# Fused multi-query attention with a residual: the upper query blocks are stored in reversed order, and the opening loads and a few early steps are put in another order

## The chip, the core and the metric

The kernel runs on one core of a Trainium2 chip. The core has five engines that work from instruction queues of their own and wait for each other by semaphores: TensorE (PE in the profile, with its weight loads shown as PEld), VectorE (DVE), ScalarE (ACT), GpSimd (POOL) and SyncE (SP). Here SyncE does nothing but issue DMA transfers, in the order in which the program lists them. The metric is the device time of one execution in microseconds; lower is better. The time shown for the kernel before is the median of three runs.

## The reference

All arrays are float32 apart from the mask. `x` is 64 x 128 x 512: 64 batches of 128 tokens.

```python
xn  = layernorm(x, g_in)
q   = (xn @ Wq) per head * 64**-0.5     # 16 heads of 64
k, v = split(xn @ Wkv)                  # one head of 64, shared by all 16 (multi-query)
k, v = [null_k; k], [null_v; v]         # a null key and value in front, from cond_64[0:2]
sim = q @ k.T + bias                    # bias: a null column, then 16 x 128 x 128
sim = causal mask, then the key mask of the batch
attn = softmax(sim)
out = layernorm((attn @ v, heads side by side) @ Wo, g_out)
return x + out
```

Two facts matter below. The attention is causal: query i uses keys 0 to i and the null key. And it is block-causal in blocks of 32: query block 0 needs key block 0, query block 3 needs key blocks 0 to 3.

## The kernel before

**Groups and steps.** The 64 batches are worked on one at a time in `step(n)`; each step is written out by hand as one order of instructions for all engines (`step_a` for even n, `step_b` for odd n, `last_step` for the last six). The projections are made for a group of four batches (GB = 4): while step n does the attention of batches n to n + 2, it also makes a quarter of the queries, keys and values of the group that is wanted about six batches later (`g, f = divmod(n + 6, GB)`). With f = 3 the group is complete, and its keys and values go through DRAM to the partitions where they are wanted (`keys_T`, `values_spread`), and its key mask is made (`mask_neg`). The query projection and the output projection use seven products of halves in place of eight (`product`, `out_product`).

**Attention of one batch.** Queries of 8 heads by 128 tokens are packed onto 128 partitions as (u, i, q): u is a half of the head pairs, i one of two blocks of 32 queries, q a query in its block. The free dimension holds, for each of 8 heads, 64 keys for the *lower* queries (tokens 0 to 63; constant `LK`) and 128 keys for the *upper* queries (tokens 64 to 127; `UK`). So partition row group s = 2u + i (32 partitions) holds lower query block i and upper query block 2 + i. The order in `region(n)` is: `scores` of the lower half of batch n + 2 (PE, line 515), `scores_add` (DVE, line 528), `values` of batch n (PE, line 606), then `scores` of the upper half of n + 2, which overwrites the same PSUM tile `ps`, and so must wait until `scores_add` has read it. `scores_add` itself adds onto the tile `s` that `bias_add` (POOL, line 494) has filled with bias and mask.

**values.** The transposed softmax weights `sb` hold, in each row group, six blocks of 32 keys: slots 0 and 1 for the lower query block, 2 to 5 for the upper one. For key block j and row group s a matmul with 32 rows and 64 columns of weights is issued for each half r of the heads, at `tile_position=(s * Q, r * DH)`: eight small tiles of the array. Where both query blocks of the row group need key block j (`both`) it streams 256 columns, otherwise 128 for the upper block alone. A row group with i = 0 needs 1 + 3 key blocks, one with i = 1 needs 2 + 4. `values_out` (ACT, line 622) moves the four PSUM tiles `po` to `oT`.

**Where the token order is set.** `xT[g]` holds the normalised tokens with features on partitions. For the first two groups `norm_T` makes it by PE transposes and one ACT copy from PSUM for each batch (line 290); for the others `tokens_T` does 32 x 32 transposes on DVE (line 299), and `tokens_out` and `tokens_in` go through DRAM. Queries, keys and values all come from `xT`, so its order of tokens is theirs. The bias is loaded once by `load_bias` into `biasp` in the order of the queries, and `causal` (POOL, line 196) writes -1e38 where a key lies after its query.

**Opening.** Batches 0 to 3 are loaded first, then the weights; `load_second` issues what follows on SP's queue. Of each batch, `norm_stats`, `norm_apply` and `norm_T` must be done before its keys and values (`kv_mm`, `kv_out`). In PSUM, `norm_T` and `kv_mm` take turns on the two buffers of `ps_w`. `norm_apply` is on DVE for batches 0 to 3 and on ACT from batch 4 on (line 278). `rstd` is made on POOL (line 257), whose queue also holds `causal`.

Of the kernel before, what the change touches and what calls it, by code (L numbers as in the profile page):

```python
# [17 lines left out]
def kernel(  # L18
# [76 lines left out]
    ROW = 1 + NL + N + 1  # L95
    LK, UK = slice(1, 1 + NL), slice(1 + NL, 1 + NL + N)
    assert NQ == GB and NQ == KC
    EPS = 1e-5
    NEG = -1.0e38
    XB = 3  # L100
# [36 lines left out]
    def load_mask(g):  # L137
        m8s[g] = gp.tile([P, TOK], U8, tag="m8", name=f"m8_{g}")
        nc.sync.dma_start(
            out=m8s[g],  # L140
            in_=mask[g * GB : (g + 1) * GB].rearrange("b n -> (b n)").partition_broadcast(P),
        )
# [23 lines left out]
    nc.sync.dma_start(out=wkv, in_=w_kv.rearrange("(kc p) f -> p kc f", p=P))  # L166

    def load_second():
        load_bias(1)
        nc.sync.dma_start(out=nbh, in_=null_bias.partition_broadcast(P))  # L170
        nc.sync.dma_start(
            out=nkv, in_=cond[0:2].rearrange("r d -> (r d)").partition_broadcast(P)
        )
        load_bias(0)
        load_mask(0)
        for r in range(2):
            nc.sync.dma_start(
                out=nv2[r * DH : (r + 1) * DH, :], in_=cond[1].unsqueeze(1)
            )
        for m in range(XB + 1, 2 * GB):  # L180
            load_x(m)
        load_mask(1)

    def load_bias(u):
        rows = slice(u * DH, (u + 1) * DH)
        bias_r = attn_bias.rearrange("(u f r) i j -> u r i f j", u=2, r=2)[u]
        for r in range(2):
            rf = slice(r * NF, (r + 1) * NF)
            nc.sync.dma_start(out=biasp[rows, rf, LK], in_=bias_r[r, 0:DH, :, 0:NL])
            nc.sync.dma_start(out=biasp[rows, rf, UK], in_=bias_r[r, DH:N])  # L190

    def causal(u):

        rows = slice(u * DH, (u + 1) * DH)
        for keys, base in ((LK, 0), (UK, DH)):
            nc.gpsimd.affine_select(
                biasp[rows, :, keys],
                biasp[rows, :, keys],
                pattern=[[0, R8], [-1, keys.stop - keys.start]],
                compare_op=ALU.is_ge,  # L200
                fill=NEG,
                base=base,
                channel_multiplier=1,
            )
# [77 lines left out]
    def norm_T(m):  # L282
        g, t = divmod(m, GB)
        if t == 0:
            xT[g] = gp.tile([P, GB, KC, N], FP, tag="xT", name=f"xT_{g}")
        xh = xs.pop(m)
        pt = ps_w.tile([P, KC, P], FP, tag="w", name=f"pxT_{m}")
        for kc in range(KC):
            nc.tensor.transpose(pt[:, kc, :], xh[:, kc * P : (kc + 1) * P], ident)
        nc.scalar.copy(xT[g][:, t], pt)  # L290

    xbs = {}

    def tokens_T(m):

        g, t = divmod(m, GB)
        if t == 0:
            xbs[g] = hp.tile([P, NQ, KC, NQ, Q], FP, tag="xb", name=f"xb_{g}", bufs=1)
        nc.vector.transpose(
            xbs[g][:, :, :, t, :].rearrange("p j c q -> p c j q"),  # L300
            xs.pop(m).rearrange("p (c j k) -> p c j k", c=KC, k=Q),
        )

# [34 lines left out]
    def kv_out(m, pkv):  # L338
# [7 lines left out]
            ALU.subtract,  # L346
        )

    def values_spread(g):

        vd = dp.tile([P, GB * DH], FP, tag="vd", name=f"vd_{g}")
        nc.sync.dma_start(out=vd, in_=kvts[g][:, 1].rearrange("p t d -> p (t d)"))
        vr[g] = hp.tile([P, NQ, GB, DH], FP, tag="vr", name=f"vr_{g}")
        src = vd.rearrange("(j p) e -> p j e", p=Q)
        for s in range(NQ):
            nc.sync.dma_start(
                out=vr[g][s * Q : (s + 1) * Q].rearrange("p j t d -> p j (t d)"),
                in_=src,
            )

    def keys_T(g):

        kb = hp.tile([P, 2, GB, Q], FP, tag="kb", name=f"kb_{g}", bufs=1)
        nc.vector.transpose(
            kb,
            kvts[g][:, 0].rearrange("p t (c k) -> p c t k", k=Q),
        )
        kd = dp.tile([P, 2, GB * Q], FP, tag="kd", name=f"kd_{g}")
        nc.sync.dma_start(
            out=kd.rearrange("p c e -> p (c e)"), in_=kb.rearrange("p c t q -> p (c t q)")  # L370
        )
        kT[g] = hp.tile([P, NQ, GB, Q], FP, tag="kT", name=f"kT_{g}")
        src = kd.rearrange("(i p) c e -> c p i e", p=Q)
        for s in range(NQ):
            nc.sync.dma_start(
                out=kT[g][s * Q : (s + 1) * Q].rearrange("p i t q -> p i (t q)"),
                in_=src[s % 2],
            )
# [90 lines left out]
    def q_out(g, c, toks, tag, name=None):  # L469
        lo = toks.start // N  # L470
        o = q_part(g, c, lo, lo + 2)
        p = prod[tag].rearrange("p (t h i) -> p t h i", t=2, h=2)
        if name is None:
            nc.scalar.copy(o, p)  # L474
        else:
            k = kept.pop(name).rearrange("p (t h i) -> p t h i", t=2, h=2)
            nc.vector.tensor_tensor(o, p, k, ALU.add)  # L477
# [108 lines left out]
    def values(b):  # L586

        g, t = divmod(b, GB)
        sb = sbs.pop(b)
        po = [  # L590
            (ps_w if s % 2 else ps_q).tile(
                [P, 2, NF, Q], FP, tag="w" if s % 2 else "ac"[s // 2], name=f"po_{b}_{s}"
            )
            for s in range(NQ)
        ]
        for j in range(NQ):
            for s in range(NQ):
                i = s % 2
                if j > 2 + i:
                    continue  # L600
                quad = slice(s * Q, (s + 1) * Q)
                both = j <= i
                slots = slice(j, j + 3, 2) if both else slice(2 + j, 3 + j)
                for r in range(2):
                    rows = slice(r * DH, (r + 1) * DH)
                    nc.tensor.matmul(  # L606
                        po[s][rows] if both else po[s][rows, 1:2],
                        vr[g][quad, j, t, :],
                        sb[quad, slots, r * NF : (r + 1) * NF, :],
                        start=(j == 0),  # L610
                        stop=True,
                        skip_group_check=(j > 0),
                        tile_position=(s * Q, r * DH),
                    )
        pos[b] = po

    def values_out(b):

        oT[b] = bp.tile([P, NC, N], FP, tag="oT", name=f"oT_{b}")
        for s, po in enumerate(pos.pop(b)):  # L620
            u, i = divmod(s, 2)
            nc.scalar.activation(  # L622
                oT[b][:, u * NF : (u + 1) * NF, :].rearrange(
                    "p f (h i q) -> p i h f q", h=2, i=2
                )[:, i],
                po,
                AF.Identity,
                bias=nv2,
            )
# [150 lines left out]


    def weights_q(kc):
        if kc in (2, 0):
            nc.vector.tensor_scalar(
                wq[:, kc, :], wq[:, kc, :], gin8[:, kc : kc + 1], None, ALU.mult
            )
        else:
            nc.scalar.activation(
                wq[:, kc, :], wq[:, kc, :], AF.Copy, scale=gin8[:, kc : kc + 1]
            )  # L790
# [32 lines left out]
    def step_a(n):  # L823
# [4 lines left out]
        first, third = paired(p12), paired(p4)  # L828
        e, nb = n + 1, n + 2
        soft = 0 < n  # L830
        if q and f == 0 and g + 1 < NG:
            load_mask(g + 1)
        if third:
# [109 lines left out]
        if n == -2:  # L943
            scores(1, 1)
            scores_add(1, 1)
            late_max.append(1)
        for m in (n + 12, n + 13):
            if m < B and n:
                load_x(m)

    def step_b(n):

# [52 lines left out]
        if q:  # L1005
            product(g, f, 7, ps_q, "a", start=False)
            keep("a", "u3")
            q_out(g, HC + f, hi_t, "c", "u3")
            if kv_late:
                kv_out(n + 6, keys_values())  # L1010
            if n == 1:
                out_mm(0)
# [29 lines left out]
        if q:  # L1042
            product(g, f, 4, ps_q, "a", start=False)
            q_out(g, HC + f, lo_t, "a")
            if f == 3:
                keys_T(g)
                values_spread(g)
                if g < NG:
                    mask_neg(g)
        if second:  # L1050
            out_product(p, 3, ps_y, "Y", start=False)
# [102 lines left out]
    norm_stats(3)  # L1154
    q_half(0, 0)
    norm_apply(2)
    norm_T(2)
    q_half(1, 0)
    norm_apply(3)
    norm_T(3)  # L1160
    weights_kv()
    norm_stats(4)
    norm_apply(4)
    q_half(2, 0)
    causal(1)
    norm_stats(5)
    norm_apply(5)
    null_shift(1)
    q_half(3, 0)
    norm_T(4)  # L1170
    for m in range(GB):
        kv_out(m, kv_mm(m))
    norm_stats(6)
    norm_stats(7)
    norm_nmr(6)
# [18 lines left out]
    weight_sum(4)  # L1194
    for c in range(4):
        q_half(c, 1)
    load_late()
    load_x(8)
    load_x(9)
# [75 lines left out]
```

## Time and profile before

| | |
|---|---|
| median of three runs | 1103.41 us (1102.82 to 1104.4) |
| the profiled execution, its own time | 1104.52 us |
| its span from first to last instruction | 1102.7 us |
| busy, share of the span | PE 98%, PEld 82%, DVE 73%, ACT 63%, POOL 64% |
| DMA moved | 105.03 MB, mean 95 GB/s |
| costliest PE groups of the chain that ended last | query products (line 456, by tile) 17%, 8% and 5%; output products (line 689) 16%, 7% and 4%; scores 9%; values 7% |
| granted clock of PE | 0.50 from 27.0 to 30.0 us, from 107.5 to 110.5 us and from 134.7 to 137.7 us; 1.00 in nearly all of the rest |

How to read it: times in the views are microseconds from the start of the span. A group of instructions is shown as line, engine, operation, tile written and tile read, sizes (partitions x elements), how many, and their time. One float32 matmul of the program stands in the trace as two records. A bracket such as `[4.50 <-ACT x L278]` says that the engine had been idle for 4.50 us, and that the instruction of that engine and line ended the wait. In a table of stretches, the columns after the length are the busy times of PE, PEld, DVE, ACT and POOL with their instruction counts, then the granted clock of PE as a share of full speed, the busy share of the DMA engines, and GB/s.

### The profile page before, as it was taken

How to read it: one execution, taken by the hardware profiler on the slowest of the kernel's cores; microseconds unless marked ns; L12 is line 12 of the kernel's file. 1: busy time of each engine (PE TensorE's matmuls, PEld its weight loads, DVE VectorE, ACT ScalarE, POOL GpSimd, SP SyncE). 2: the span in 40 equal slices, each digit the busy share in tenths (PEclk: the TensorE clock that was granted, in tenths of full speed). 3: DMA queues.
4: the chain of work that ended last, by engine and by line, in shares of the span. 5: the costliest groups of instructions: out<-in, count | busy, mean ns of one | idle time of the engine just before them, and what ended most of it. 6: DMA issues, size and time to landing. Idle time of an engine off the chain costs nothing.

```text
span 1102.7 us, 29987 instructions
## 1 busy us (share of the span) xinstructions
PE 1077.4 (98%) x11780; PEld 900.2 (82%) x11780; DVE 800.9 (73%) x1545; ACT 694.9 (63%) x2779; POOL 702.1 (64%) x517
## 2 busy tenths in 40 slices
PE   7999999999999999999999999999999999999997
PEld 6876788888888888888888888888888888888653
DVE  4667578786787878678687787878678787657772
ACT  3355566666766666666666676666676666567682
POOL 2465757676675766757586675767667576665572
PEclk9999999999999999999999999999999999999999
DMA  7414242333334242333324234233333424111211
GB/s 198 139 44 120 77 117 76 112 90 111 82 100 122 70 120 78 118 97 92 105 80 133 69 90 133 70 118 89 112 84 99 121 67 125 58 59 41 68 60 67
DMA packets 67980, 105.03 MB, mean 95 GB/s; under 512 B 8448, under 2 KB 32640, under 8 KB 66048
## 3 DMA queue, kind: packets, MB, share of 16 engines
q1 hardware_dynamic: 67024, 102.07, 31.1%
q8 instruction: 92, 1.51, 0.6%
q10 hardware_dynamic: 816, 1.05, 0.3%
q14 instruction: 48, 0.39, 0.1%
HBM read 67.45 MB, written 35.65 MB: 93 GB/s over the span
## 4 chain that ended last, share of the span: by engine, by line
PE 86%; DVE 7%; ACT 4%; DMA 2%; issue 1%; POOL 0%; SPq 0%; DVEq 0%; ACTq 0%
PE pa L456 17%; PE pyX L689 16%; PE ps L515 9%; PE pc L456 8%; PE pyY L689 7%; PE po L606 7%; PE pkv L327 6%; PE py L636 5%; PE pw L456 5%; PE pyw L689 4%; DVE mneg L485 3%; ACT s L542 3%; PE pq L405 2%; ACT x L278 1%; DVE s L528 1%; DMA x<-in_x_dram 1%
## 5 line engine op out<-in xcount | busy, mean ns | idle before, releaser
L542 ACT ACTIVATE s<-s,nmax 128x65 f32<-128x65 f32 (+1 forms) x1024 | 372.5, 370 | 6.1 <-DVE nmax L533 6.1
L563 POOL TENSOR_TENSOR s<-s,rinv 128x512 f32<-128x512 f32 (+1 forms) x128 | 189.2, 1478 | 184.1 <-DVE rinv L559 177.3
L494 POOL TENSOR_TENSOR s<-biasp,mneg 128x1552 f32<-128x1552 f32 x64 | 206.1, 3220 | 105.4 <-DVE sb L578 103.0
L542 ACT ACTIVATION_READ_ACCUMULATOR s<-s,nmax 128x1 f32 x1024 | 197.6, 193 | 0.0
L622 ACT ACTIVATE oT<-po,nv 128x256 f32<-128x256 f32 x256 | 100.2, 474 | 139.5 <-PE po L606 139.5
L528 DVE TENSOR_TENSOR s<-ps,s 128x512 f32<-128x512 f32 (+1 forms) x128 | 119.9, 936 | 64.9 <-PE ps L515 64.9
L689 PE MATMUL pyX<-wT,oT 128*128 128x256 f32 x672 | 163.2, 386 | 0.0
L689 PEld LDWEIGHTS pyX<-wT,oT 128*128 128x128 f32 x672 | 124.5, 191 | 22.8 <-issue 4.8
L515 PEld LDWEIGHTS ps<-kT,qT 64*64 64x64 f32 x4096 | 90.9, 133 | 40.7 <-issue 29.6
L456 PE MATMUL pa<-xS,wq 128*128 128x256 f32 x480 | 123.5, 380 | 0.0
L533 DVE TENSOR_REDUCE nmax<-s 128x8 f32<-128x520 f32 (+1 forms) x128 | 122.1, 954 | 1.4
L515 PE MATMUL ps<-kT,qT 64*64 64x64 f32 (+1 forms) x4096 | 115.1, 250 | 5.6 <-DVE s L528 4.1
L578 DVE STREAM_TRANSPOSE sb<-s 128x1536 f32<-128x1536 f32 x64 | 113.5, 1773 | 8.0 <-POOL s L563 3.8
L456 PEld LDWEIGHTS pa<-xS,wq 128*128 128x128 f32 x480 | 91.4, 191 | 12.6
L606 PE MATMUL po<-sb,vr 32*64 32x128 f32 (+1 forms) x3584 | 99.7, 322 | 0.3 <-ACT qT L474 0.3
L606 PEld LDWEIGHTS po<-sb,vr 32*64 32x64 f32 x3584 | 79.4, 131 | 10.9 <-DVE y L760 0.8
L467 ACT COPY ku<-pa 128x256 f32<-128x256 f32 x120 | 44.7, 372 | 65.4 <-PE pa L456 64.1
L477 DVE TENSOR_TENSOR qT<-pc,ku 128x256 f32<-128x256 f32 x120 | 49.7, 414 | 42.6 <-ACT ku L467 35.3
L327 PE MATMUL pkv<-wkv,xT 128*128 128x128 f32 x512 | 73.6, 290 | 1.0 <-ACT xT L290 1.0
L327 PEld LDWEIGHTS pkv<-wkv,xT 128*128 128x128 f32 x512 | 67.3, 199 | 8.0 <-issue 5.2
L278 ACT ACTIVATE x<-x,nmr,rstd 128x512 f32<-128x512 f32 x60 | 48.5, 814 | 32.6 <-DVE nmr L265 31.7
L456 PE MATMUL pc<-xT,wS 128*128 128x256 f32 x240 | 62.0, 381 | 3.6 <-DVE qT L477 3.5
(95 smaller groups left out, 1926.7 us busy)
## 6 DMA issues: line engine op xcount, KB each, us to landing
x<-in_x_dram SPq DMA_DIRECT2D x64, 256.0 KB
res<-in_x_dram SPq DMA_DIRECT2D x64, 256.0 KB
out_dram<-y SPq DMA_DIRECT2D x64, 256.0 KB
xd<-xb SPq DMA_DIRECT2D x14, 1024.0 KB
xT<-xd SPq DMA_DIRECT2D x56, 256.0 KB
vr<-vd SPq DMA_DIRECT2D x64, 128.0 KB
kT<-kd SPq DMA_DIRECT2D x64, 64.0 KB
kd<-kb SPq DMA_DIRECT2D x16, 128.0 KB
```

The costliest lines, as they stand in the source:

```text
L327: nc.tensor.matmul(pkv, xT[g][:, t, kc, :], wkv[:, kc, :], start=(kc == 0), stop=(kc == KC - 1),)
L456: nc.tensor.matmul(prod[tag], w[:, kc, f * P : (f + 1) * P], t[:, :, kc, :], start=(start and kc == 0), stop=(kc == HK - 1), skip_group_ch ...
L494: nc.gpsimd.tensor_tensor(S[b], biasp, mneg[:, t].unsqueeze(1).broadcast_to([P, R8, ROW]), ALU.add,)
L515: nc.tensor.matmul(pv[u * DH : (u + 1) * DH, r, f, :], qT[g][rows, f, t, hf, u], kT[g][rows, 0 : nk // Q, t, :], start=True, stop=True,)
L528: nc.vector.tensor_tensor(sv, pss.pop((b, hf)), sv, ALU.add)
L533: nc.vector.tensor_reduce(nmax[b][:, hf], S[b][:, :, WITH_NULL[hf]], AX.X, ALU.max, negate=True)
L542: nc.scalar.activation(row, row, AF.Exp, bias=nmax[b][:, hf, k : k + 1], accum_out=rsum[b][:, hf, k : k + 1],)
L563: nc.gpsimd.tensor_tensor(sv, sv, rinvs.pop((b, hf)).unsqueeze(2).broadcast_to([P, R8, sv.shape[2]]), ALU.mult,)
L578: nc.vector.transpose(sb.rearrange("p j e q -> p e j q"), S[b][:, :, 1 : ROW - 1].rearrange("p e (j k) -> p e j k", k=Q),)
L606: nc.tensor.matmul(po[s][rows] if both else po[s][rows, 1:2], vr[g][quad, j, t, :], sb[quad, slots, r * NF : (r + 1) * NF, :], start=(j == 0),
L622: nc.scalar.activation(oT[b][:, u * NF : (u + 1) * NF, :].rearrange("p f (h i q) -> p i h f q", h=2, i=2)[:, i], po, AF.Identity, bias=nv2,)
L689: nc.tensor.matmul(prod[key], h[:, c, :], w[:, c, :], start=(start and c == 0), stop=(c == HC - 1), skip_group_check=not start,)
```

## The change

The upper queries of a row group are stored in reversed block order: row groups with i = 0 get lower block 0 and upper block 3, those with i = 1 get lower block 1 and upper block 2. Each then needs five key blocks. `values` issues its 14 pairs of matmuls in a list written out for that. The order is made where `xT` is written (three ACT copies in place of one for the first eight batches; another place in the DVE transpose for the others), `load_bias` and `causal` follow it in more pieces, keys and values are brought back to the order of the tokens on their way through DRAM (three DMAs in place of one for each), and `values_out` puts the blocks back with another stride.

Apart from that, batch 4 is loaded at the head of `load_second`, batches 5 to 7 ahead of the second bias half, and the null value later; one of the four query weight scalings goes from ACT to DVE; `norm_T(2)` and `norm_T(3)` stand one projection later and `null_shift(1)` after the keys and values of the first group; the mask of group 1 is made earlier in step 1; and in `step_a` the two loads of `x` stand at the beginning and no longer at the end.

```diff
+    PLACE = 0, 1, 3, 2
     def load_second():
+        load_x(XB + 1)
         load_bias(1)
...
+        for m in range(XB + 2, 2 * GB):
+            load_x(m)
         load_bias(0)
         load_mask(0)
+        load_mask(1)
+
+    def load_null_value():
         for r in range(2):
             nc.sync.dma_start(
                 out=nv2[r * DH : (r + 1) * DH, :], in_=cond[1].unsqueeze(1)
             )
-        for m in range(XB + 1, 2 * GB):
-            load_x(m)
-        load_mask(1)
...
-            nc.sync.dma_start(out=biasp[rows, rf, UK], in_=bias_r[r, DH:N])
+            for i, at in enumerate((N - Q, N - 2 * Q)):
+                nc.sync.dma_start(
+                    out=biasp[u * DH + i * Q : u * DH + (i + 1) * Q, rf, UK],
+                    in_=bias_r[r, at : at + Q],
+                )
     def causal(u):
-        rows = slice(u * DH, (u + 1) * DH)
-        for keys, base in ((LK, 0), (UK, DH)):
+        for rows, keys, base in (
+            (slice(u * DH, (u + 1) * DH), LK, 0),
+            (slice(u * DH, u * DH + Q), UK, N - Q),
+            (slice(u * DH + Q, (u + 1) * DH), UK, N - 2 * Q),
+        ):
...
-        nc.scalar.copy(xT[g][:, t], pt)
+        for at, to, n in ((0, 0, 2), (3, 2, 1), (2, 3, 1)):
+            nc.scalar.copy(
+                xT[g][:, t, :, to * Q : (to + n) * Q], pt[:, :, at * Q : (at + n) * Q]
+            )
...
-            xbs[g][:, :, :, t, :].rearrange("p j c q -> p c j q"),
+            xbs[g][:, :, :, PLACE[t], :].rearrange("p j c q -> p c j q"),
...
+    def to_tokens(out, places):
+        for at, to, n in ((0, 0, 2), (2, 3, 1), (3, 2, 1)):
+            nc.sync.dma_start(
+                out=out[to * Q : (to + n) * Q], in_=places[at * Q : (at + n) * Q]
+            )
...
-        nc.sync.dma_start(out=vd, in_=kvts[g][:, 1].rearrange("p t d -> p (t d)"))
+        to_tokens(vd, kvts[g][:, 1].rearrange("p t d -> p (t d)"))
...
-        for j in range(NQ):
-            for s in range(NQ):
-                i = s % 2
-                if j > 2 + i:
-                    continue
+        order = [(0, s) for s in range(NQ)] + [(1, s) for s in range(NQ)]
+        order += [(2, 0), (2, 2), (3, 0), (2, 1), (3, 2), (2, 3)]
+        for j, s in order:
+            i = s % 2
...
+            blocks = slice(i, 4 - i, 3 - 2 * i)
                 oT[b][:, u * NF : (u + 1) * NF, :].rearrange(
-                    "p f (h i q) -> p i h f q", h=2, i=2
-                )[:, i],
+                    "p f (s q) -> p s f q", q=Q
+                )[:, blocks],
...
     def weights_q(kc):
-        if kc in (2, 0):
+        if kc != 1:
...
     def step_a(n):
+        for m in (n + 12, n + 13):
+            if m < B and n:
+                load_x(m)
...
-        for m in (n + 12, n + 13):
-            if m < B and n:
-                load_x(m)
     def step_b(n):
...
+            if n == 1:
+                mask_neg(g)
...
                 values_spread(g)
-                if g < NG:
+                if n > 1:
                     mask_neg(g)
...
     q_half(0, 0)
     norm_apply(2)
+    norm_apply(3)
+    q_half(1, 0)
     norm_T(2)
-    q_half(1, 0)
-    norm_apply(3)
-    norm_T(3)
     weights_kv()
     norm_stats(4)
     norm_apply(4)
     q_half(2, 0)
+    norm_T(3)
     causal(1)
     norm_stats(5)
     norm_apply(5)
-    null_shift(1)
     q_half(3, 0)
     norm_T(4)
     for m in range(GB):
         kv_out(m, kv_mm(m))
+    null_shift(1)
...
+    load_null_value()
     load_late()
```

## The prediction

> **What bounds the kernel now.** I read the page first, then the stretches, then the order of PE's work in time, and last the chain.
>
> ```profile
> PE 1077.4 (98%) x11780; PEld 900.2 (82%) x11780; DVE 800.9 (73%) x1545; ACT 694.9 (63%) x2779; POOL 702.1 (64%) x517
> 237.00:499.00 262.00, 261.48 (x2946) 224.95 (x2945) 201.43 (x397) 174.22 (x697) 175.19 (x129) 1.00 0.34 99
> 27.00:30.00 3.00, 2.22 (x10) 2.22 (x11) 1.52 (x3) 0.72 (x2) 0.00 (x0) 0.50 0.00 0
> 107.50:110.50 3.00, 3.00 (x11) 2.55 (x10) 2.93 (x6) 1.34 (x9) 0.20 (x1) 0.50 0.40 106
> 134.70:137.70 3.00, 3.00 (x9) 2.38 (x8) 1.49 (x4) 1.86 (x9) 2.94 (x2) 0.50 0.31 131
> ```
>
> In the steady part PE is idle for 0.5 of 262 us: there only less PE time counts. Elsewhere there are three stretches at half clock; these are PE's waits ahead of them:
>
> ```profile
> 24.62 0.66 PE L289 MATMUL pxT<-ident,x 128*128 128x128 f32 x4 [4.50 <-ACT x L278]
> 27.78 5.03 PE L327 MATMUL pkv<-wkv,xT 128*128 128x128 f32 x24 [0.98 <-ACT xT L290]
> 105.74 1.10 PE L515 MATMUL ps<-kT,qT 64*64 64x128 f32 x32 [2.45 <-DVE s L528]
> 133.40 1.13 PE L456 MATMUL pc<-xT,wS 128*128 128x256 f32 x4 [2.29 <-DVE qT L477]
> ```
>
> The attention of two neighbouring steady steps, 24 and 25:
>
> ```profile
> 483.38 0.69 PE L515 MATMUL ps<-kT,qT 64*64 64x64 f32 x32
> 484.00 1.56 PE L606 MATMUL po<-sb,vr 32*64 32x256 f32 x56
> 485.49 1.10 PE L515 MATMUL ps<-kT,qT 64*64 64x128 f32 x32
> 501.19 1.56 PE L606 MATMUL po<-sb,vr 32*64 32x256 f32 x56
> 502.87 1.10 PE L515 MATMUL ps<-kT,qT 64*64 64x128 f32 x32
> ```
>
> `values` takes 1.49 us from its start to the next start at 484.00, and 1.68 at 501.19. The second is a step with f = 3; the chain tells what ended it:
>
> ```profile
> 499.32 2.89 DVE mneg L485 x2
> 502.22 0.61 DVE s L528
> 502.83 0.04 issue
> 502.87 1.10 PE ps L515 x32
> ```
>
> The mask on DVE makes `scores_add` late by 0.2 us. In the other steps nothing waits there.
>
> **Part 1, values.** Four full matmuls of 256 columns take 1.73 us in the chain (1.69 ns a column). A row group with i = 1 streams 2 x 256 + 2 x 128 = 768 columns per half r: 1.30 us, plus 0.19 to the next form, is the 1.49 seen. So both halves and all four row groups run side by side, and the longest row group sets the time; the single records agree, with 0.216 us between passes of 256 columns in one tile while eight tiles run. After the change each row group has 640 columns: 128 x 1.69 = 0.216 us less, to 1.27. Bounds: 0, if the new order lets one group wait for another, and 0.41, if the 0.19 to the next form went too. I take 0.216: the tiles' starts in the trace do not follow the program's order across row groups, so none waits for another.
>
> [...]
>
> Where it counts: of 64 batches not in the 12 steps with f = 3 from 5 to 49 (1.68 us there; DVE's chain begins at PE's `pyX` of the same step, so PE only waits 0.4 in place of 0.2), nor in batches 60 and 61, where the chain runs over DVE and ACT from 1058.3 to 1068.1. 50 x 0.216 = 10.8 us. `values_out` starts 0.43 nearer to PE's end, since row group 0 ends last too; ACT's four moves (1.57 us) still end over 1 us ahead of the `kv` and `pa` that want the buffers.
>
> **Part 2, the opening.** Before, PE is done with the fourth query tile at 20.14 and reaches the fifth at 32.81: 12.67 us for 0.44 + 4 x 0.87 = 3.92 us of work. `x` of batch 4 is issued at 18.79, behind eight bias DMAs and two of the null value (2.39 us), and read at 21.67. Now it is issued at 6.9 in place of the first bias DMA, behind `wkv`, which lands at 13.7; so by about 14.4. Then:
> - DVE scales a third weight (0.75 us) when it lands (10.83): `norm_stats(2)` starts at 11.6, not 10.46, and all to `wkv` 1.16 later (15.76). PE does not see it: its first query tile waits for ACT's scaling at 13.32 as before.
> - Batch 4, with the gaps it had from 21.67 to 24.56: statistics 15.76, POOL 17.0 to 17.55, ACT 17.85 to 18.65. PE, with two transposes moved back, reaches `norm_T(4)` at 19.85, no wait; first keys 20.3 to 21.17.
> - The second keys need the buffer that ACT's `xT` copies of batch 4 free. On ACT `norm_apply(5)` is ahead of them; it needs POOL's `rstd`, behind `causal(1)`, now in three pieces (0.66 + 1.09 + 1.09, to 20.35). From the end of `causal` to PE it was 25.25 to 27.78, 2.5 us; three copies take about 0.2 more than one (0.58 us for 128 x 512, 0.37 for 256, so 0.27 for 128, partly overlapped): 23.05. PE waits 1.9 us and is done with the keys at 25.65.
> - `null_shift(1)` (1.92) now lies between `kv_out` and `norm_stats(6)`, which starts at 27.9; ACT's `norm_apply(6)` ended 3.06 after that start (33.06 to 36.12): 30.95. PE is there at 29.55: waits 1.4. `norm_T(6)` at 31.0 is 5.7 us ahead of the 36.7 before.
> - Behind it, mask, `bias_add(0)` (4.04) and DVE's weight sums (1.2 + 4.1 + 2.2) end at about 43, when the first `scores` end (48.56 less 5.7): level. The three `kd` DMAs and `kT` land by 37. The null value (2.39 on SP) delays `wo` and batches 8 and 9, wanted some 9 us later. From there PE, ACT and DVE follow each other as before.
>
> Gain 5.7. Bounds: 8.75, all of the excess; and about 2, if both waits bring half clock again (1.7 each, as in part 3).
>
> **Part 3, step 1.** Mask 1 moves from 101.8 to 94.5, ahead of a wait of 3.56 us on DVE (to 100.35) that takes up its time; POOL's last read of the old mask ends at 92.8. `values` to `scores`, 4.01 us at 101.73, becomes 1.49 (counted above down to 1.27): 2.5, and the half clock from 107.28 to 110.69 goes: 3.41 / 2 = 1.7. Sum 4.2; at least 2.5.
>
> [...] The records here show half clock after 2.45 and 2.29 us, and they decide.
>
> **Part 4, loads of x.** In step 2 they were issued at 122.5, behind the store, and landed at 131.9 (DVE waits 2.06 and 1.45 for them, PE 2.29). Now they are issued after `vr` (110.0), need no buffer that is still in use, and land ahead of 125. 2.4 plus 1.7 = 4.1. Bounds 0 (another wait there) and 4.5. In later steps they free only DVE waits that PE does not see.
>
> **Part 5, what is added.** Keys and values back to token order: three DMAs for one, twice in each of 16 groups. SP's queue moves by 2 x 0.33 + 2 x 0.43 = 1.5 us, and `kv_out` of the next group, which overwrites the source, must wait for the third `vd`:
>
> ```profile
> 502.92 0.43 SPq L352 DMA_DIRECT2D vd<-kvt  x1
> 506.11 1.73 SPq L356 DMA_DIRECT2D vr<-vd  x4
> 508.60 0.28 DVE L342 TENSOR_TENSOR kvt<-pkv,nkv 128x128 f32<-128x128 f32 x1
> ```
>
> `vr` starts when `vd` has landed, `kvt` 2.5 us later; over the groups the margin is 2.06 to 3.9. So 1.5 is hidden, 0.5 left: cost 0. `kT` and `vr` are wanted a step or more later. Four more bias DMAs and the last `causal` pieces lie under PE's work of the opening.
>
> **Part 6, the tail.** PE's wait at 1066.5 (1.61 us, no half clock) grows by 2 x 0.216 to 2.04. Waits of 1.61 and 2.29 lie on two sides of what halves the clock; 2.04 is nearer to the second: cost 1.7, or 0.
>
> **Sum.** 10.8 + 5.7 + 4.2 + 4.1 - 1.7 = 23.1 us. The profiled execution took 1104.52 (span 1102.7 and 1.8 around it): 1081.4. The median is 1.1 below it: 1080.3.
>
> **Rivals.**
> - *The opening trades its wait for others.* For: two waits of 1.4 and 1.9 are foreseen, both behind POOL's and DVE's queues. At half clock or with DMAs landing later it gives 0 to 3: 1083 to 1086.
> - *`values` does not get shorter where it counts*: another queue order, or DVE takes PE's place in more steps (it is busy for 77% of the steady part). Against: in the other steps `scores` start 0.2 us after the last matmul starts, with no wait. All lost, and with it the tail's longer wait: 1080.3 + 10.8 - 1.7 = 1089.4, and less where only some steps lose it.
> - *Slower: `kv_out` waits for `vd` on DVE.* Behind it DVE holds `q_out` and with that PE's buffers. It has to cost 23.1 / 14 = 1.7 us in each of 14 groups; from a wait of that size half clock doubles it, some 1104 to 1128. The third `vd` would have to land 4 us later than now, not 1.5.
> - *Better*: no wait at 21.2, none in the tail: 1073 to 1077.
>
> **How the numbers follow.** Forecast (1077 to 1083) 0.54; opening 0.18; values 0.14; slower 0.05; better 0.09. 1075 to 1089.5 leaves out the slower case, some of the better and a little of the third: under 0.15, as the chances are themselves rough. A measurement of this kernel can tell about 0.2%, 2.2 us; faster 0.94, same 0.01, slower 0.05.
>
> **What would show it.** 1.27 us from `values` to `scores` in steps without a mask, 1.68 with f = 3; no idle PE from 20.1 to 21.1, then waits of 1 to 2 us; clock 1.00 in all of 25 to 138; no `kvt` on DVE ended by a DMA. It is wrong if `values` stays at 1.49, or if PE shows new waits in each group.

## The result, and the profile after

The changed kernel takes 1092.03 us (median of four runs, 1090.72 to 1093.44); the kernel before, on the same chip, 1103.91 us. The ratio is 0.9894, 95% interval 0.9875 to 0.9912: faster by 11.9 us, about half of the 23.1 that the prediction summed up, and outside its range (1075 to 1089.5). The profiled execution took 1093.44 us, with a span of 1090.7 us, 12.0 less than before.

The page's busy times of the changed kernel:

```profile
PE 1072.2 (98%) x11780; PEld 896.5 (82%) x11780; DVE 797.6 (73%) x1546; ACT 694.6 (64%) x2794; POOL 703.5 (65%) x519
```

The same stretches that the prediction showed (the first one is chosen anew, where the half clock lies now; columns: length, busy times of PE, PEld, DVE, ACT and POOL, granted clock, DMA share, GB/s):

```profile
23.60:27.00 3.40, 3.33 (x15) 3.33 (x16) 0.29 (x1) 0.01 (x1) 0.00 (x0) 0.50 0.19 26
107.50:110.50 3.00, 3.00 (x16) 2.64 (x15) 1.23 (x5) 2.25 (x12) 3.00 (x2) 1.00 0.51 143
134.70:137.70 3.00, 3.00 (x18) 2.69 (x18) 2.93 (x9) 2.10 (x12) 2.75 (x3) 1.00 0.63 132
237.00:499.00 262.00, 261.46 (x2946) 224.83 (x2946) 201.15 (x398) 174.43 (x698) 175.06 (x130) 1.00 0.33 99
```

The half clock at 107 and at 135 us is gone (the column before the last two is 1.00), PE is as full in the steady part as before, and one window of half clock remains in the opening. PE's order in time, changed kernel, opening:

```profile
20.23 1.06 PE L341 MATMUL pkv<-wkv,xT 128*128 128x128 f32 x8
23.67 4.52 PE L341 MATMUL pkv<-wkv,xT 128*128 128x128 f32 x24 [2.38 <-ACT xT L302]
33.67 0.55 PE L300 MATMUL pxT<-ident,x 128*128 128x128 f32 x3 [1.59 <-ACT x L289]
```

The wait of 4.50 us ahead of the fifth query tile is gone; in its place stand 2.38 us ahead of the second keys and 1.59 us ahead of `norm_T(6)`, the two places that the prediction named. Further on, the same view of the two places that had a wait, `scores` in step 1 and the query product `pc` in step 3:

```profile
98.81 1.55 PE L623 MATMUL po<-sb,vr 32*64 32x256 f32 x56
100.28 1.10 PE L533 MATMUL ps<-kT,qT 64*64 64x128 f32 x32
...
122.22 1.89 PE L707 MATMUL pyX<-wT,oT 128*128 128x256 f32 x8
123.95 1.03 PE L474 MATMUL pc<-xT,wS 128*128 128x256 f32 x4
```

`scores` follow `values` by 1.47 us with no wait, and `pc` has none either. And in the steady part, steps 24 and 25:

```profile
472.58 1.55 PE L623 MATMUL po<-sb,vr 32*64 32x256 f32 x56
474.05 1.10 PE L533 MATMUL ps<-kT,qT 64*64 64x128 f32 x32
...
489.75 1.55 PE L623 MATMUL po<-sb,vr 32*64 32x256 f32 x56
491.44 1.10 PE L533 MATMUL ps<-kT,qT 64*64 64x128 f32 x32
```

This is the surprise. In the step without a mask, `values` takes 1.477 us from its start to the next start, not 1.27; before it took 1.486 (medians over the 64 batches). With f = 3 it stays at 1.68. Worked out from the starts of `values` in both traces, the 12.0 us come from:

| stretch | before | after | gain |
|---|---|---|---|
| start to the first `scores` | 47.88 | 45.06 | 2.8 |
| step 1 (second to third `values`) | 17.93 | 13.86 | 4.1 |
| step 3 (third to fourth `values`) | 21.43 | 17.18 | 4.2 |
| all other steps together | | | 0.9 |

Of the last row, `values` itself makes up about 0.45 us (50 x 0.009); the rest was not followed up.

### The profile page after: what moved, and what is told of

Its sections match the earlier page's. It is cut to its first block, busy times and chain, and to the rows that moved or that the text cites. A ratio compares the mean times of both kernels' runs of the same rounds, so it can differ in the third digit from the quotient of the medians.

```text
span 1090.7 us, 30112 instructions
## 1 busy us (share of the span) xinstructions
PE 1072.2 (98%) x11780; PEld 896.5 (82%) x11780; DVE 797.6 (73%) x1546; ACT 694.6 (64%) x2794; POOL 703.5 (65%) x519
## 4 chain that ended last, share of the span: by engine, by line
PE 86%; DVE 7%; ACT 4%; DMA 2%; issue 1%; POOL 0%; ACTq 0%; SPq 0%; DVEq 0%; POOLq 0%
PE pa L474 18%; PE pyX L707 16%; PE ps L533 9%; PE pc L474 8%; PE pyY L707 7%; PE po L623 7%; PE pkv L341 6%; PE py L654 5%; PE pw L474 5%; PE pyw L707 4%; DVE mneg L503 3%; ACT s L560 2%; PE pq L423 1%; DMA x<-in_x_dram 1%; ACT x L289 1%
## 5 line engine op out<-in xcount | busy, mean ns | idle before, releaser
L764 DVE TENSOR_TENSOR yn<-yn,gob 128x512 f32<-128x512 f32 x56 | 39.2, 700 | 36.3 <-ACT yn L761 36.3
```

## The experiments

The first theory was that the row group whose pair stands last in the list, (2,3), gets its weights late. A record is one entry of the trace, a weight load or a pass (the streaming of one matmul's columns); in batch 24 the 28 float32 matmuls of `values` stand as 56 loads and 56 passes. In the records of batch 24 the last pass of `values` starts at 1.280 us, where 640 columns would have it near 1.075. The rival: 56 passes have a fixed price of 26.4 ns each, whatever their order.

### Other orders of the last pairs

```diff
-        order += [(2, 0), (2, 2), (3, 0), (2, 1), (3, 2), (2, 3)]
+        order += [(2, 0), (2, 1), (2, 2), (2, 3), (3, 0), (3, 2)]
```

> Same matmuls as in the changed kernel, but the last six pairs of values are issued key block by key block, as the loop of the kernel before had them: (2,0), (2,1), (2,2), (2,3), (3,0), (3,2). Theory (what holds values at 1.477 us is the place of the pair (2,3) at the end of the list: its weights are loaded late, and its last pass starts at 1.280 us where 1.075 was due): the pair now stands fourth, values takes 1.28 to 1.40 us from its start to the next form, and the profiled time falls by 4 to 10 us. Rival (56 passes with a weight load each, 26.4 ns a pass, whatever their order and length): 1.477 us as before, no change in time.

Measured (one run): `values` 1.476 us, 1090.86 us in all. The pair (2,3) in fourth place helps nothing.

```diff
-        order += [(2, 0), (2, 2), (3, 0), (2, 1), (3, 2), (2, 3)]
+        order += [(2, 0), (2, 2), (3, 0), (2, 1), (2, 3), (3, 2)]
```

> The changed kernel with only the last two pairs of values exchanged: (2,3) ahead of (3,2). Theory (the pair issued last pays, whichever it is): row group 2 takes the place of row group 3; values falls little, to between 1.35 and 1.477 us, and the last passes in the records are now those of (3,2). If it is the tile of row group 3 that is slow and not the last place, it falls to 1.28. Rival (56 passes at 26.4 ns): 1.477 us.

Measured (one run): 1.476 us, 1090.32 us. The two results speak against row group 3 as the cause, and alone they would fit the rival. The next one does not.

```diff
-        order = [(0, s) for s in range(NQ)] + [(1, s) for s in range(NQ)]
-        order += [(2, 0), (2, 2), (3, 0), (2, 1), (3, 2), (2, 3)]
+        order = [(0, s) for s in range(NQ)]
+        order += [(1, 0), (2, 1), (1, 2), (2, 3)]
+        order += [(2, 0), (1, 1), (2, 2), (1, 3), (3, 0), (3, 2)]
```

> The row groups with i = 1 get their single key block second and their second full one third, so that all eight tiles stream 256, 128 columns side by side before they part: after (0,s) come (1,0), (2,1), (1,2), (2,3), then (2,0), (1,1), (2,2), (1,3), (3,0), (3,2). Theory (issue order, late weight loads of the last pair): nothing is issued far ahead of its turn, values takes 1.27 to 1.32 us, which is 0.16 to 0.21 less in 50 batches, 8 to 10 us: 1082 to 1084 us. Rival (56 passes at 26.4 ns each): 1.477 us and the time of the changed kernel, 1092.

Measured (four runs): `values` 1.345 us, 1085.99 us (ratio to the kernel before 0.9835, 0.9813 to 0.9857). The same 56 passes take 0.13 us less, so the fixed price falls; but 1.345 is not the 1.27 to 1.32 of the first theory, and in the first two orders the last place alone cost the same 1.476 whichever pair stood there. The order matters, by a rule that was not yet found.

The records gave it. `values` has 14 pairs, and each pair is eight records in program order: weight load and pass twice for the one half r, then for the other. I number them 1 to 112 and match the records to pairs by their order and length (the trace doesn't name the pair). In the three orders with 1.477 us, the load of the last pair's second half, record 109, starts at 1.117 or 1.118 us, although its tile could have taken it from about 0.75 on. Record 44, the second pass of the first half of the full pair (1,1), ends at 1.086 or 1.087: 31 ns earlier. Another load in all of them, record 69, starts at 0.671 to 0.673, and record 4 ends at 0.640 or 0.641: 31 or 32 ns again. So the new theory, read from these starts and ends: in `values`, PE sees no more than 64 records from the oldest that has not ended. Load 109 then comes into view when all up to 45 have ended, load 69 when all up to 5 have; of these, 44 and 4 are the last to end. The late loads bound the number: with 66 records in view load 109 would not have been held by record 44, and with 63 load 107 would have been held too, but in the three orders only two loads start after 1.087 (1.118 and 1.173 in the changed kernel), by the program's order 109 and 111. A table of starts worked out from this rule and the records' own durations gives 1.345 for the lockstep order, the measured time; but it was made after that run. The sharp test is then to change which record is late:

```diff
-        order = [(0, s) for s in range(NQ)] + [(1, s) for s in range(NQ)]
-        order += [(2, 0), (2, 2), (3, 0), (2, 1), (3, 2), (2, 3)]
+        order = [(0, s) for s in range(NQ)] + [(1, 0), (1, 2), (1, 1), (1, 3)]
+        order += [(2, 0), (2, 2), (3, 0), (2, 1), (2, 3), (3, 2)]
```

> The changed kernel with values in the order: first key blocks (0,0) to (0,3), then (1,0), (1,2), (1,1), (1,3), (2,0), (2,2), (3,0), (2,1), (2,3), (3,2). Theory now (queue of 64): PE sees at most 64 records of its program from the oldest one that has not ended, so record n can start only when record n - 64 has ended. In the three orders with 1.477 us, record 109, the load of the second half of the last pair, starts at 1.117, 31 ns after record 44 ended at 1.086, and that is the second pass of the first half of (1,1), a full pass. With the short pairs (1,0), (1,2) ahead, record 44 is a short pass and ends by 0.89. A table worked out with this rule and the durations in the records (0.216 and 0.109 us a pass, 0.05 for a load that is not hidden, 0.158 from the end of streaming to the end of a record) gives 1.345 for the lockstep order and here 1.28 to 1.30 us. Rival (what matters is that the tiles have passes of equal length side by side): this order mixes full and short passes as the one with 1.477, so it stays at 1.45 to 1.48. Steps with a mask stay at 1.68.

Measured (one run): 1.283 us in the steps without a mask, 1083.22 us. And the opposite:

```diff
-        order = [(0, s) for s in range(NQ)] + [(1, s) for s in range(NQ)]
-        order += [(2, 0), (2, 2), (3, 0), (2, 1), (3, 2), (2, 3)]
+        order = [(0, s) for s in range(NQ)] + [(1, 1), (1, 3), (1, 0), (1, 2)]
+        order += [(2, 0), (2, 2), (3, 0), (2, 1), (2, 3), (3, 2)]
```

> The opposite order of the second key blocks: (1,1), (1,3) ahead of (1,0), (1,2), then (2,0), (2,2), (3,0), (2,1), (2,3), (3,2). Theory (queue of 64): records 36 and 40 are now the ones that end late (1.086 and 1.093), so that all from record 100 on, that is a part of the last two pairs, can start only at 1.12 to 1.15: values takes 1.50 to 1.54 us, longer than in the kernel before, although no tile has more to stream. The time rises by 50 x 0.03 to 50 x 0.06, 1.5 to 3 us. Rival (equal lengths side by side): 1.45 to 1.48, no change.

Measured: 1.510 us, above the 1.486 of the kernel before; 1091.88 us in all (one run); from the first to the last `values` 992.9 us against 991.2 with the first of the other orders (natural in the table below), whose opening is alike. Both fall into the intervals set before, and the rival (equal lengths side by side) is wrong for both: these orders mix full and short passes just as the one with 1.477 does. PE's order in time, first the order with the short pairs ahead, in steps 24 and 25, then step 24 of the opposite one:

```profile
469.18 1.35 PE L623 MATMUL po<-sb,vr 32*64 32x256 f32 x56
470.46 1.10 PE L533 MATMUL ps<-kT,qT 64*64 64x128 f32 x32
...
486.16 1.35 PE L623 MATMUL po<-sb,vr 32*64 32x256 f32 x56
487.83 1.10 PE L533 MATMUL ps<-kT,qT 64*64 64x128 f32 x32 [0.33 <-DVE s L546]
```

```profile
471.02 1.58 PE L623 MATMUL po<-sb,vr 32*64 32x256 f32 x56
472.53 1.10 PE L533 MATMUL ps<-kT,qT 64*64 64x128 f32 x32
```

The second column is the length of the group: 1.35 against 1.55 of the changed kernel and 1.58. In step 25, which has f = 3, PE is ready earlier and waits 0.33 us for DVE in place of working; nothing is gained there. The records of batch 24 (nanoseconds from the start of `values`):

```
order                  late record        ends   next load held back   starts   last pass starts   values
changed kernel         44, full pass      1086   109                   1118     1280               1477
natural                44, full pass      1086   109                   1117     1280               1477
swapped                44, full pass      1087   109                   1118     1280               1478
lockstep               44, short pass      873   none (all by 1011)             1118               1345
short pairs first      44, short pass      886   none (all by 978)              1085               1282
full pairs first       36, full pass      1086   101                   1117     1312               1510
before                 44, full pass      1086   109                   1117     1292               1489
```

The rows stand in the order of the runs above. The last row tells why the profile before misled: the late load at 1117 is there too, but the tile that it belongs to was busy until 1183, so it cost nothing. With 640 columns in every row group, as in the first three rows, the last pass stands behind it.

### The front alone, and the reversed blocks alone

The kernel before with only the new order of the opening (the third weight scaling on DVE with it), the early mask and the early loads; the diff is shown in part:

```diff
     def load_second():
+        load_x(XB + 1)
         load_bias(1)
...
+            if n == 1:
+                mask_neg(g)
...
+        for m in (n + 12, n + 13):
+            if m < B and n:
+                load_x(m)
```

> The kernel before with only the new front, that is the order of the opening loads and steps, the mask of group 1 made earlier and the loads of x at the head of step_a; no block is reversed, values, bias, causal and the ways through DRAM are those of before. Theory (the gain of 11.9 us is 2.8 of the opening, 4.1 of step 1 and 4.2 of step 3, while the reversed blocks give 50 x 0.01 = 0.5 only): 1092.0 to 1093.5 us. Rival (the reversed blocks give a good part of it): 1095 us or more.

Measured (four runs): 1089.82 us, ratio 0.9868 (0.9852 to 0.9884). Less than expected, and less than the whole change (0.9875 to 0.9912; the intervals overlap a little): the reversed blocks, as they are made here, do not give 0.5 us but seem to cost. The place is the opening:

```profile
20.56 4.14 PE L330 MATMUL pkv<-wkv,xT 128*128 128x128 f32 x32
...
30.17 0.66 PE L292 MATMUL pxT<-ident,x 128*128 128x128 f32 x4 [1.58 <-ACT x L281]
...
41.56 0.64 PE L518 MATMUL ps<-kT,qT 64*64 64x64 f32 x28
```

The keys of all four batches run in one group of 32 with no wait, and the first `scores` start at 41.56, not 45.06. DVE's queue tells the difference, first in the kernel with the front alone, then in the changed kernel:

```profile
15.65 0.69 DVE L255 BATCH_NORM_STATS2 st<-x 128x6 f32<-128x512 f32 x1
17.61 0.68 DVE L255 BATCH_NORM_STATS2 st<-x 128x6 f32<-128x512 f32 x1
```

```profile
15.33 0.69 DVE L263 BATCH_NORM_STATS2 st<-x 128x6 f32<-128x512 f32 x1
19.86 0.69 DVE L263 BATCH_NORM_STATS2 st<-x 128x6 f32<-128x512 f32 x1 [2.49 <-DMA x<-in_x_dram]
```

The second row is batch 5. With the reversed layout each half of the bias is six transfers and not four; batch 5 stands behind them on SP (issued at 14.54 and not 13.19) and lands 2.49 us after DVE could use it. The same from the other side, the kernel before with only the reversed blocks (its diff is the one above without the front):

> The kernel before with only the reversed blocks: PLACE, the bias and causal in pieces, the copies of xT, the three DMAs for one, the list in values, values_out; the front is that of before. Theory (the reversed blocks bring 50 x 0.01 = 0.5 us in values and lose more in the opening, where batch 4 is loaded behind six bias transfers, not four, and POOL has a third piece of causal ahead of rstd): values 1.477 us, first scores at 48.5 to 51 us in place of 47.88, so 1104 to 1107 us, as slow as before or slower by up to 0.25%. Rival (the layout costs nothing by itself, its loss in the changed kernel comes only from the new order of loads): first scores at 47.9, 1103.5 or less.

Measured over twelve runs: 1107.06 us, ratio 1.0017 (1.0005 to 1.003): slower by 0.2%. `values` 1.476 us as in the changed kernel; the first `scores` at 50.46, and the old wait grown:

```profile
26.26 1.11 PE L297 MATMUL pxT<-ident,x 128*128 128x128 f32 x4 [6.17 <-ACT x L286]
```

It was 4.50 us before. So the reversed blocks as written gain under 1 us in `values` and lose more in the opening: 2.6 us here, and 3.5 between the kernel with the front alone and the profiled changed kernel, of which 1.7 is half clock. The front alone carries the whole gain.

### The opening, mended

```diff
         load_x(XB + 1)
+        load_x(XB + 2)
         load_bias(1)
...
-    causal(1)
     norm_stats(5)
+    causal(1)
...
-    null_shift(1)
     norm_stats(6)
...
     values_spread(0)
+    null_shift(1)
     null_shift(0)
```

> The changed kernel with three steps of the opening moved: batch 5 is loaded straight after batch 4, ahead of the bias; causal(1) stands after norm_stats(5), so that POOL makes rstd of batch 5 first; null_shift(1) stands after values_spread(0), behind the statistics of batches 6 and 7. Theory (the reversed layout lost some 3 us in the opening, since two more bias transfers and a third piece of causal stand ahead of batch 5): PE's wait of 2.38 us ahead of the second keys and the half clock after it go, and the wait of 1.59 us ahead of norm_T(6) too; the first scores start at 39.4 to 41 us in place of 45.06, 1086 to 1088.5 us in all. Rival (the bias, the mask and the weight sums on POOL and DVE take over as the limit): PE waits at the second scores instead and 1 to 2 us are gained, 1090 to 1091.

Measured (four runs): 1087.76 us, ratio 0.9851 (0.9827 to 0.9875); both waits are gone and no window of half clock is left in the opening:

```profile
20.57 3.91 PE L342 MATMUL pkv<-wkv,xT 128*128 128x128 f32 x32
...
28.20 0.60 PE L301 MATMUL pxT<-ident,x 128*128 128x128 f32 x4
...
39.54 0.69 PE L534 MATMUL ps<-kT,qT 64*64 64x64 f32 x32
40.16 1.99 PE L424 MATMUL pq<-xT,wq 128*128 128x256 f32 x8
```

The first `scores` start at 39.54 and not 45.06: 5.5 us in the profiled runs, as expected; 1.7 of it is the half clock that the profiled changed kernel has there, and the medians differ by 4.3. The rival's wait at the second `scores` did not come. The three moves were made together; how much each is worth by itself was not measured.

### Steps 1 and 3

Each of the two parts taken back alone, the mask behind `values_spread` again, and the loads at the end of the step again:

```diff
-            if n == 1:
-                mask_neg(g)
...
-                if n > 1:
+                if g < NG:
                     mask_neg(g)
```

> The changed kernel with the mask of group 1 made again behind keys_T and values_spread of step 1, as before. Theory (part 3): the second values takes 4.0 us to the next form and not 1.48, one window at half clock follows, from the second to the third start of values 17.9 us in place of 13.86; the time 4.1 us above the changed kernel. Rival (the earlier opening alone would have ended this wait): 13.9 to 15 us.

Measured (one run, 1094.47 us in all): second to third `values` 17.91 us, as in the kernel before, and the wait is back:

```profile
96.71 1.55 PE L623 MATMUL po<-sb,vr 32*64 32x256 f32 x56
100.72 1.10 PE L533 MATMUL ps<-kT,qT 64*64 64x128 f32 x32 [2.46 <-DVE s L546]
```

```diff
-        for m in (n + 12, n + 13):
-            if m < B and n:
-                load_x(m)
         if q and f == 0 and g + 1 < NG:
...
             late_max.append(1)
+        for m in (n + 12, n + 13):
+            if m < B and n:
+                load_x(m)
```

> The changed kernel with the two loads of x of step_a at the end of the step again, as before. Theory (part 4 of the prediction: in step 3 PE waits for them and then runs at half clock): from the third to the fourth start of values 21.4 us in place of 17.18, half clock for one window of 3.41 us near 125 us, the other steps as in the changed kernel; the time 4.2 us above it. Rival (it was the earlier mask that ended the wait of step 3): 17.2 us and no change.

Measured (one run, 1096.46 us in all): third to fourth `values` 23.21 us, 6.0 more than the changed kernel and not 4.2:

```profile
124.83 2.08 PE L474 MATMUL pc<-xT,wS 128*128 128x256 f32 x4 [2.71 <-DVE qT L495]
```

The wait is 2.71 us where it had been 2.29, and the half clock lasts two windows of 3.41 us (124.24 to 131.07) and not one; in the first of them PE is idle for 0.6 us (the last section comes back to this). The cause is the one predicted: DVE waits 2.40 and 1.54 us for the two loads of x. The two totals are only 2.4 and 4.4 us above that of the changed kernel, as the profiled openings differ: the first `scores` start at 42.96 and 43.05 here, without half clock, and at 45.06 there.

### Together, and the mask

The order with the short pairs ahead and the mended opening, in one kernel:

> Both together: the order of values with the short second blocks first, and the three moved steps of the opening. Theory: the gains add, 50 x 0.19 = 9.5 us and 4 to 5.7 us below the changed kernel: 1076 to 1080 us. Rival for the sum: with values shorter, DVE ends later than PE in more steps than those with a mask, and only a part of the 9.5 us comes: 1081 to 1086.

Measured (four runs): 1079.48 us, ratio 0.9769 (0.9753 to 0.9786), inside 1076 to 1080: the gains add. PE's waits in this kernel (total, how many, the longest):

```profile
PE ps L534 <- DVE s L547: 6.1, 13, 2.2
```

Twelve of the 13 are the f = 3 steps. There DVE's mask is the end, as the prediction had said of those steps; so the mask was split (`slice(0, 1)` is the part with 64 keys, `slice(1, 2)` the one with 128):

```diff
+        if q and f == 3 and n > 1:
+            mask_neg(g, slice(0, 1))
         if soft_hi:
             rinv(e, 1)
             scale(e, 1)
...
                 if n > 1:
-                    mask_neg(g)
+                    mask_neg(g, slice(1, 2))
```

> The kernel of opening_and_small_first, and in the 12 steps with f = 3 the smaller part of the mask (64 keys) is made ahead of rinv and scale of the upper half, only the larger behind keys_T. Theory (in these steps DVE is late by the mask: scores_add ends 0.4 us after PE could use it): 1.0 of the 2.97 us of mask moves into DVE's idle time ahead of rinv (0.83 us), values goes from 1.68 to 1.28 us in these steps too, 12 x 0.4 = 4.7 us less: 1074 to 1076 us. Rival (what is pushed back on DVE, rinv and with it scale on POOL, comes late for the transposes of the weights): less than 2 us, 1077.5 to 1080.

Measured (four runs): 1074.32 us, ratio 0.972 (0.9703 to 0.9737); `values` takes 1.283 us in the 12 steps too, and of the waits one is left:

```profile
PE ps L534 <- DVE s L547: 2.2, 1, 2.2
```

In such a step DVE now waits for PE, 0.39 us, where PE had waited for DVE:

```profile
474.99 0.29 DVE L504 TENSOR_SCALAR mneg<-m 128x256 f32<-128x256 uint8 x1
...
476.57 1.69 DVE L504 TENSOR_SCALAR mneg<-m 128x512 f32<-128x512 uint8 x1
478.65 0.69 DVE L547 TENSOR_TENSOR s<-ps,s 128x512 f32<-128x512 f32 x1 [0.39 <-PE ps L534]
```

The smaller piece takes 0.29 us here where 1.0 had been assumed from 2.97 for both; the two pieces together take 1.98. The traces show what goes with it: in the kernel without the split the smaller piece takes 1.55 us in these steps, with POOL's `scale` running beside it for 1.4 us, and 0.28 us at 33.6, where POOL does nothing. After the split no POOL instruction runs beside it; the larger piece, now beside `scale`, takes 1.69 us, and 0.41 us at 33.3, where it is alone. The changed kernel shows the same: the smaller piece takes 1.56 us at 487.80, beside `scale`, and the two take 0.28 and 0.41 us at 37.80 and 38.00, where POOL is idle. So the two pieces also got shorter, by 0.99 us together, which the expectation had not counted on; how much of the gain is due to that was not measured.

## Why the prediction was right and wrong

| part | predicted | measured |
|---|---|---|
| 1, `values` | 10.8 | 0.9 at most (0.45 in `values`) |
| 2, opening | 5.7 | 2.8 |
| 3, step 1 | 4.2 | 4.1 |
| 4, loads of x | 4.1 | 4.2 |
| 5, added DMAs | 0 | 0 |
| 6, tail | -1.7 | 0 |
| sum | 23.1 | 12.0 |

**Part 1 failed, and it is nearly the whole miss.** The failing step is the sentence "the tiles' starts in the trace do not follow the program's order across row groups, so none waits for another". The first half is true. The second does not follow: passes overtake each other in the records of batch 24, and still load 109 starts at 1.118 us, 32 ns after record 44 has ended (1.086). The bound was written down (0, "if the new order lets one group wait for another"), and the wrong end of it taken. Right in this part: the 0.216 us of streaming were there to be had (1.283 us with the short pairs ahead, against 1.27 forecast), and the 12 steps with f = 3 stay at 1.68 because of DVE's mask, as the split mask showed.

The records of `values` fit a view of 64 records, counted from the oldest that has not ended: load 109, held by record 44, and load 107, not held, leave 64 or 65, and two times forecast with 64 were met (1.28 to 1.30 us against 1.283 measured, 1.50 to 1.54 against 1.510). This is a reading of the records of `values` alone.

**Part 2 was mis-sized.** Both waits came where it put them, 2.38 us (1.9 forecast) and 1.59 (1.4). The first has another cause than the one named: it was to be POOL, behind the third piece of `causal(1)`; in the trace POOL is done with `causal(1)` at 20.05, is idle for 1.06 us and then makes `rstd`, because DVE had waited 2.49 us for batch 5 from DRAM (shown above):

```profile
21.11 0.55 POOL L268 TENSOR_TENSOR rstd<-rstd,nhalf 128x1 f32<-128x1 f32 x1 [1.06 <-DVE rstd L267]
```

That part of the layout's cost, batch 5 behind two more bias transfers, was not in the sum. With it PE was idle for 2.31 of the 3.41 us from 20.18 to 23.60, and the 3.41 us after that ran at a clock of 0.50, which is 1.7 us lost; the prediction had kept that as its lower bound. Without that window the first `scores` start at 42.8 to 43.4, a gain of 4.5 to 5.1 us: of the eight profiles with this opening (the changed kernel, the five other orders and the two kernels with one part taken back) three have it and five not. So 1.7 of the 2.9 us that this part missed come in some profiles of the same opening and not in others: in the natural order the wait is 1.96 us, to 23.57, and the clock 1.00 from 20 to 34 us; in the lockstep order it is 1.93 us, to 23.85, and the clock 0.77 from 23 to 27 and 0.74 from 27 to 30.

**Parts 3 and 4 held.** The two parts, taken back one at a time, bring back 4.05 and 6.0 us.

**Part 5** held in its cost, 0: from 100 to 925 us the changed kernel shows no wait of PE. The margin of 0.5 us was not there, though: DVE's `kvt` at 628.3 us waits 0.18 us for the DMA of `vd`, where the prediction named "no `kvt` on DVE ended by a DMA" as a sign of being right. In the kernel with the mended opening one such wait is 1.69 us (at 102.6), and PE shows none behind it either.

**Part 6** has no case here, since `values` did not get shorter: the wait near the end is 1.58 us, at full clock. In the three kernels with 1.283 it is 2.23 to 2.25, and two of the three show the window of half clock behind it, as part 6 had taken for a wait of 2.04.

The rival "`values` does not get shorter where it counts: another queue order" named the right mechanism with 0.14, and the rival on the opening the other one; they came together, which no case allowed for. 1092 lies 2.6 above the 1089.4 of that rival alone.

## What to carry to other kernels

Where small matmuls of unequal length share the array, try the order of the program even though passes overtake each other: here order alone made `values` 1.283, 1.477 or 1.510 us. Count the records (two loads and two passes for each float32 matmul in these traces) and put the ones that end early first, so that no long pass stands where record 44 stood, 65 places ahead of the load 109 that started 31 ns after its end. An idle resource in the trace before can be the next bound: the late weight load at 1117 ns, whose tile was busy until 1183, cost nothing before, and with 640 columns in every row group it was followed by the last pass. And look at what a layout's extra transfers do where the queue is full: here six bias transfers in place of four put batch 5 at 14.54 us and not 13.19 on SP, and the first `scores` at 45.06 and not 41.56. Take the layout apart from the rest of a change and measure both.

## What the runs showed that was not expected

- In `values` two loads start 31 or 32 ns after the record that stands 65 places ahead of them in the program has ended: load 69 after record 4 (0.641 to 0.672 in every order), and load 109 after record 44 (101 after 36 with the full pairs ahead) in every order where that one ends late (1.086 to 1.117). A view of 64 records from the oldest unfinished one would do that; it is the author's reading.
- In batch 24, before and after, the first two passes of 256 columns of a tile start 0.267 us apart, later ones 0.216. That the 0.05 us between them are the second load, which is not hidden there, is the author's estimate.
- A wait of PE cost more than its length in some places and not in others. In the profiles before and after, from the first clock record (at 4.88 and 6.53 us) on, the clock changes after 3.41 us or whole multiples of it: at half clock 6.83, 3.41 and 3.41 us before and 3.41 after, with 75.09, 23.89 and 962.56 us of full clock behind them before and 1061.55 after. Cut into such windows of 3.41 us, ahead of PE's last work, those at full clock with 1.87, 2.23, 2.31 and 2.67 us of idle PE are followed by half clock; those with 1.58, 1.59, 1.62 and 1.83 us, and all with less, are not. The window at half clock with 0.98 us of idle PE (25.36 to 28.77, before) is followed by another, as is the one with 0.6 in the run with the loads put back; the other four in the profiles before and after, with 0.07 us or less, by full clock. That the 1.96 us of the natural order fell across a border of two windows, and so left the clock at 1.00, is the author's reading.
- A gain can be missing without any new wait in the profile: of 10.8 us at most 0.9 came, and `values` shows no idle time, only a group of 1.55 us where the order with the short pairs ahead measured 1.35. The single records show it.
